# A fixed order for the first keys of an attention and FFN kernel, and its output weights queued behind a copy

## The chip, the cores and the metric

The kernel runs on one core of a Trainium2 chip. A core has five engines that take part: TensorE (PE; its weight loads are shown as PEld), VectorE (DVE), ScalarE (ACT), GpSimd (POOL) and SyncE (SP), which here only issues DMAs. The metric is the device time of one execution in microseconds (us); lower is better.

## What is computed

The reference, cut to what matters:

```python
def attention(hidden_q, hidden_kv, mask, bias):         # h = 32 heads of dh = 128
    q = (hidden_q @ Wq).reshape(b, lq, h, dh)
    k = (hidden_kv @ Wk).reshape(b, lk, h, dh)
    v = (hidden_kv @ Wv).reshape(b, lk, h, dh)
    score = einsum('bqhd,bkhd->bhqk', q, k) / sqrt(dh) + bias
    probs = where(mask, softmax(where(mask, score, -inf)), 0)
    return einsum('bhqk,bkhd->bqhd', probs, v).reshape(b, lq, h * dh) @ Wo

def ffn(x):                                             # 8 experts of rank 16
    base_out = x @ base_W.T + base_b
    topk_p, topk_i = top_k(softmax(x @ router_W.T + router_b), 8)
    w = sum_over_k(topk_p * onehot(expert_map[topk_i]))
    return base_out + einsum((x @ A) * w, B) * 2

x = x + attention(layernorm(x), ctx, mask, bias)        # x, ctx: 16 x 64 x 512, fp32
x = x + ffn(layernorm(x))
```

There are 1024 tokens of width 512. The weights Wq, Wk and Wv are 512 x 4096, Wo is 4096 x 512.

## The kernel before

**Products.** Every large fp32 product is made from two halves of each operand: `split` (L69-71) casts the source to a reduced fp32 on ScalarE (the high part, names ending in `h`) and subtracts it from the source on VectorE (the low part, names ending in `l`). `mm3` then issues three matmuls, high by high, low by high and high by low (L262). On top of it the projections of queries, keys and values use a form of Winograd's scheme: both operands are cut into 2 x 2 blocks, and seven products of sums of blocks take the place of eight products of blocks. `winograd` (L213-257) issues the products in the order 1, 2, 6, 5, 7, 4, 3. The sums of token blocks are made by `Tokens.make` (L136-146; names `tt`, `t1` to `t7`), those of key weights by `Weights.make` (L164-173; `s`, `gh`, `gl`), those of value weights by `OctWeights.make` (L198-206). Product 6 needs two sums on each side (s1, then s2), 5 uses the first of them, 7, 4 and 3 need a third or fourth. After a product, `post` copies PSUM banks on ScalarE (`u`, `u2`, `u3`, `c21`) or adds them on VectorE (`c11`, `c22`, `c12`), and the results are stored in DRAM by DMA (`kd` for keys, `vd` for values).

**Stages.** A quad is four heads. The first stage makes the keys of quads 0 and 1 together. Their seven products are interleaved, quad 0 then quad 1; one product of one quad is 12 matmuls of 128 x 512. Product 1 is written out by hand on TensorE, VectorE and ScalarE (from L360). For the other six, the loop at L411-421 makes the operands of the next product for quad 0, for the tokens and for quad 1, and then steps both quads. There only TensorE's order is fixed as written (`manual_schedule` from L355). VectorE's and ScalarE's orders are made by the framework's scheduler. Then come stages of values (eight heads at a time) and of keys, each with its operands made a stage ahead. The loads of key weights use the buffers `raw` (ten), those of value weights the buffers `o` (nine), which the token sums `tt` use too.

**Pairs.** Sixteen pairs of heads follow. Each does the scores of its two heads (`S`), seven products of the queries of the next pair (`Q`), the output projection of the previous pair (`O`) and transposes of the probabilities (`T`). The string of steps is `QSQQOOQOQOOQOQOTTO`, and a pair ends with the products of probabilities and values. `scores` (L484-504) runs 16 exponentials on ScalarE for the two heads. The `Queries` products 1, 6 and 7 are copied out of PSUM by `u` (L558, ScalarE); the bank of products 1, 6, 7 and 4 is the same, so a following product cannot write it before the copy. `load_o` (L468-476) loads the two blocks of output weights of the pair (`so`, 256 KB each) and splits them into `wh` and `wl`; it stands at the third `Q` (L610-611).

**Order.** [...] Outside of `manual_schedule` the scheduler sets it from the order of the program, dependencies and its own estimates. `tc.issue_after(x)` adds an order edge: what is issued under it comes after x.

Of the kernel before, what the change touches and what calls it, by code (L numbers as in the profile page):

```python
# [15 lines left out]
ALU = mybir.AluOpType  # L16
# [20 lines left out]
ORDER = (1, 2, 6, 5, 7, 4, 3)  # L37
# [10 lines left out]
def xattn_ffn_kernel(ctx: ExitStack, tc: tile.TileContext, x, ctxT, wq, wk, wv, wo, fside, mask,  # L48
                     base_wT, base_b, arT, router_b, lora_b, expert_map, out):
    nc = tc.nc  # L50
# [58 lines left out]
    with ExitStack() as actx:  # L109
# [9 lines left out]
        class Tokens(dict):  # L119
# [13 lines left out]
                    r.append(d)  # L133
                return r

            def make(self, i):  # L136
                b, t = self.b, self.t
                if i == 6:
                    t[1] = self.diff(b[0, 1], b[0, 0], "tt1")
                    t[2] = self.diff(b[1, 1], t[1], "tt2")  # L140
                src = (b[0, 0] if i == 1 else b[1, 0] if i == 2 else t[2] if i == 6 else t[1] if i == 5 else
                       self.diff(b[1, 1], b[0, 1], "tt3") if i == 7 else
                       self.diff(b[1, 0], t[2], "tt4") if i == 4 else b[1, 1])
                self[i] = [tp.tile([P, 2, HALF], F32R, tag=f"t{i}{c}", name=f"t{i}{c}") for c in "hl"]
                for k in range(2):
                    split(self[i][0][:, k], self[i][1][:, k], src[k])
# [6 lines left out]
        class Weights(dict):  # L153
# [7 lines left out]
                self.eng.tensor_tensor(r, a, b, op)  # L161
                return r

            def make(self, i):  # L164
                a11, a12, a21, a22 = self.a
                if i == 6:
                    self.s1 = self.summed(a21, a22, ALU.add, "s1")
                    self.s2 = self.summed(self.s1, a11, ALU.subtract, "s2")
                src = (a11 if i == 1 else a12 if i == 2 else self.s2 if i == 6 else self.s1 if i == 5 else
                       self.summed(a11, a21, ALU.subtract, "s3") if i == 7 else a22 if i == 4 else  # L170
                       self.summed(a12, self.s2, ALU.subtract, "s4"))
                self[i] = [blk("g", f"g{c}", F32R, (P, 2, self.cols)) for c in "hl"]
                split(self[i][0], self[i][1], src)

# [5 lines left out]
        class OctWeights(dict):  # L180
# [25 lines left out]
                    split(self[i][0][kc], self[i][1][kc], src[kc])  # L206

            def all(self):
                for i in ORDER:
                    self.make(i)  # L210
                return self

        def winograd(mm, n, emit, yzbank=bank, order=ORDER, begun=None):  # L213

            xb, zb, yb, u, u2, u3 = ({} for _ in range(6))

            def post(i, k):
                if i == 1:  # L220
                    u[k] = blk("sn", "u")
                    nc.scalar.copy(u[k], xb[k])
                elif i == 2:
                    c = blk("ob", "c11")
                    nc.vector.tensor_tensor(c, u[k], zb[k], ALU.add)
                    emit(0, 0, k, c)
                elif i == 6:
                    u2[k] = blk("sn", "u2")
                    copied[:] = [nc.scalar.copy(u2[k], xb[k])]
                elif i == 7:  # L230
                    u3[k] = blk("sn", "u3")
                    copied[:] = [nc.scalar.copy(u3[k], xb[k])]
                    c = blk("ob", "c22")
                    nc.vector.tensor_tensor(c, u3[k], yb[k], ALU.add)
                    emit(1, 1, k, c)
                elif i == 4:
                    c = blk("ob", "c21")
                    nc.scalar.copy(c, xb[k])
                    emit(1, 0, k, c)
                elif i == 3:  # L240
                    c = blk("ob", "c12")
                    nc.vector.tensor_tensor(c, u2[k], yb[k], ALU.add)
                    emit(0, 1, k, c)

            for i in order:
                for k in range(n):
                    if i == 1:
                        xb[k] = begun[k] if begun else bank()
                    elif i == 2:
                        zb[k] = yzbank(k)  # L250
                    elif i == 5:
                        yb[k] = yzbank(k)
                    b = xb if i in (1, 6, 7, 4) else zb if i == 2 else yb
                    if i > 1 or not begun:
                        mm(i, k, b[k], i in (1, 2, 5))
                    post(i, k)
                yield i

        def mm3(o, stat, mov, first, last):
# [83 lines left out]
        def emit_k(q):  # L343
            def emit(i, j, k, c):
                stored[:] = [nc.sync.dma_start(out=kd[4 * q + 2 * i + k][:, j * HALF:(j + 1) * HALF], in_=c)]
            return emit
# [8 lines left out]
        with tc.manual_schedule(engines={nc.tensor.engine}):  # L355
# [3 lines left out]
            with tc.manual_schedule(engines={nc.tensor.engine, nc.vector.engine, nc.scalar.engine}):  # L359
# [22 lines left out]
                for q in range(2):  # L382
                    part(q, 1)
                    begin(q, 1)
            both = [winograd(mm_weights(tc_, gs[q]), 2, emit_k(q), yz, begun=xbs[q]) for q, yz in
                    enumerate((bank, lambda k: small_bank("yz")))]

            def keys_of(q, g):
# [19 lines left out]
                    q, kind = stages[n]  # L408
                    ops[n] = gran4(load_raw(wk[q]), nc.vector) if kind == "k" else OctWeights(wv[q // 2])

            for n in range(7):  # L411
                if n < 6:
                    gs[0].make(ORDER[n + 1])
                    tc_.make(ORDER[n + 1])
                    gs[1].make(ORDER[n + 1])
                else:
                    load(0)
                    load(1)
                    ops[0].all()
                next(both[0])  # L420
                next(both[1])
            for n, (q, kind) in enumerate(stages[:-1]):
                load(n + 2)
                ops[n + 1].all()
# [115 lines left out]
            class Queries:  # L540
# [6 lines left out]
                def run(self, g, order):  # L547
                    mm = mm_weights(tx, g)
                    b, s = {}, {}
                    for i in order:  # L550
                        x_ = "x" if i in (1, 6, 7, 4) else "z" if i == 2 else "y"
                        if i in (1, 2, 5):
                            b[x_] = bank()
                        mm(i, 0, b[x_], i in (1, 2, 5))
                        with tc.high_priority(offset=SOON):
                            if i in (1, 6, 7):
                                s[i] = blk("sn", "u")
                                nc.scalar.copy(s[i], b["x"])  # L558
                            if i == 4:
                                self.blocks[1, 0] = blk("ob", "q21")  # L560
                                nc.scalar.copy(self.blocks[1, 0], b["x"])
                            for at, key, u, bk in ((2, (0, 0), 1, "z"), (7, (1, 1), 7, "y"), (3, (0, 1), 6, "y")):
                                if i == at:
                                    self.blocks[key] = blk("ob", "q")
                                    add = nc.vector.tensor_tensor(self.blocks[key], s[u], b[bk], ALU.add)  # L565
                                    if i == 7:
                                        self.last = add.ins
                        yield
# [24 lines left out]
            for p in range(NP):  # L593
# [7 lines left out]
                for c in steps:  # L601
                    if c == "S":
                        ps = [scores(qs.head(i), ks[i], bms[i]) for i in range(2)]
                        if not last:
                            ks = [load_k(2 * p + 2 + i) for i in range(2)]
                            bms = [bias_of(2 * p + 2 + i) for i in range(2)]
                    elif c == "Q":
                        nxt(1)
                        n += 1
                        if n == 3:  # L610
                            w = load_o(p)
                        if n == 7 and p + 2 < NP:
                            with tc.issue_after(nxt.last):
                                after = Queries(load_pair(p + 2), ORDER)
                        if n == 7 and p + 2 == NP:
                            sar = [blk("raw", "sar", F32, (P, 2, NB)) for _ in range(2)]
                            sbw = [blk("raw", "sbw") for _ in range(KC)]
                            slb = blk("g", "slb")
                            nc.sync.dma_start(out=slb, in_=lora_b)
                            for i in range(2):  # L620
                                nc.gpsimd.memset(sar[i][:, :, NAR:NB], 0.0)
                                nc.sync.dma_start(out=sar[i][:, :, 0:NAR], in_=arT[:, 2 * i:2 * i + 2])
                            for kc in range(KC):
                                nc.sync.dma_start(out=sbw[kc], in_=base_wT[:, kc])
                    elif c == "T":
                        pts.append(transpose_p(ps[len(pts)]))
                    else:
                        proj_o(t, *prev)
                        t += 1
                        if last and t == 2:  # L630
                            w = load_o(p)
# [221 lines left out]
```

## Time and profile before

| what | us |
|---|---|
| median of three runs (lowest, highest) | 779.36 (778.44, 779.77) |
| the profiled execution | 779.6 |
| its span, first to last instruction | 777.8 |
| TensorE busy in the span | 769.8 |
| VectorE busy | 573.5 |
| ScalarE busy | 413.8 |
| GpSimd busy | 134.3 |

The mean granted TensorE clock was 0.998 of full speed. A line of the timeline reads: start, duration, engine, line of the kernel, operation, output and inputs, shape; in brackets the idle time of the engine before it and what ended it. The names in the lines are the program's tile names. A DMA's time to landing is counted from its issue.

### The profile page before, as it was taken

To read this page: it belongs to the slowest core of one execution; us is meant where nothing else is said; L and a number is where in the kernel's file an instruction comes from. 1 tells how busy PE (TensorE), PEld (TensorE's weight loads), DVE (VectorE), ACT (ScalarE), POOL (GpSimd) and SP (SyncE) were. 2 spreads that over 40 slices of the span, in tenths; PEclk is the share of its full clock that TensorE was granted. 3 is DMA by queue.
4 is the path that set the end of the run, shared out by engine and by line. 5 is a ranking of instruction groups with operands and counts; after the bars stand their busy time and mean duration, and the time that the engine had idled before them with its cause. 6 is when DMAs were issued, how large, how long until landed. Compare 5 with 4: busy or idle time off the path is not lost.

```text
span 777.8 us, 16657 instructions
## 1 busy us (share of the span) xinstructions
PE 769.8 (99%) x6306; PEld 641.6 (82%) x6306; DVE 573.5 (74%) x1037; ACT 413.8 (53%) x1166; POOL 134.3 (17%) x143
## 2 busy tenths in 40 slices
PE   8999999999999999999999999999999999999998
PEld 5888888888888888878888888888888888888897
DVE  7995566566665756788878787778777877779975
ACT  5654454545544545576564556555655565556461
POOL 0000000000000522133320332033203320210330
PEclk9999999999999999999999999999999999999999
DMA  7595646464634445574543354425542544252011
GB/s 260 192 304 177 203 154 210 134 212 151 205 119 175 150 141 198 166 245 140 184 164 126 103 180 164 140 93 177 163 143 93 175 164 143 98 170 69 1 56 55
DMA packets 74993, 120.48 MB, mean 155 GB/s; under 512 B 7712, under 2 KB 25376, under 8 KB 74912
## 3 DMA queue, kind: packets, MB, share of 16 engines
q1 hardware_dynamic: 74768, 119.36, 46.1%
q8 instruction: 49, 0.80, 0.4%
q14 instruction: 32, 0.26, 0.1%
q10 hardware_dynamic: 144, 0.06, 0.0%
HBM read 83.74 MB, written 35.65 MB: 153 GB/s over the span
## 4 chain that ended last, share of the span: by engine, by line
PE 95%; DVE 3%; DMA 1%; SPq 0%; ACT 0%; issue 0%; POOL 0%; DVEq 0%; POOLq 0%
PE ps L262 75%; PE yz L262 5%; PE ps L699 5%; PE pss L490 4%; PE ps L522 4%; PE pst L509 2%; DVE gl L71 1%; DMA cT<-in_ctxT 1%; PE pst L104 0%; DVE bs L665 0%; PE pt L104 0%; DVE tt L132 0%; DVE ol L71 0%; DVE s L161 0%; POOL st L668 0%
## 5 line engine op out<-in xcount | busy, mean ns | idle before, releaser
L70 ACT CAST gh<-s 128x512 fp32r<-128x512 f32 (+1 forms) x128 | 65.5, 515 | 90.7 <-PE ps L262 81.8
L498 ACT ACTIVATE p<-p,nm 128x64 f32<-128x64 f32 x256 | 85.5, 336 | 30.8 <-DVE nm L495 30.8
L262 PE MATMUL ps<-wh,oh 128*128 128x512 f32 x256 | 101.3, 396 | 0.0
L538 DVE TENSOR_TENSOR acc<-acc,ps 128x512 f32<-128x512 f32 x128 | 86.8, 681 | 19.2 <-PE ps L262 19.0
L71 DVE TENSOR_TENSOR gl<-s,gh 128x512 fp32r<-128x512 f32 (+1 forms) x128 | 71.6, 563 | 39.7 <-ACT gh L70 39.1
L262 PE MATMUL ps<-wh,ol 128*128 128x512 f32 x256 | 99.8, 390 | 0.0
L262 PE MATMUL ps<-wl,oh 128*128 128x512 f32 x256 | 99.8, 390 | 0.0
L161 POOL TENSOR_TENSOR s<-rq 128x256 f32<-128x256 f32 x32 | 26.1, 815 | 261.7 <-DMA rq<-in_wq 128.0
L71 DVE TENSOR_TENSOR gl<-raw,gh 128x512 fp32r<-128x512 f32 (+1 forms) x49 | 34.6, 705 | 35.4 <-ACT gh L70 25.0
L70 ACT CAST gh<-raw 128x512 fp32r<-128x512 f32 (+1 forms) x49 | 29.8, 609 | 57.2 <-PE yz L262 36.6
L262 PEld LDWEIGHTS ps<-wl,oh 128*128 128x128 f32 x256 | 48.0, 188 | 10.0
L262 PEld LDWEIGHTS ps<-wh,ol 128*128 128x128 f32 x256 | 48.1, 188 | 9.8 <-DVE ol L71 0.5
L262 PEld LDWEIGHTS ps<-wh,oh 128*128 128x128 f32 x256 | 48.1, 188 | 9.5
L481 POOL TENSOR_TENSOR bm<-bm,maskb 128x512 f32<-128x512 f32 x32 | 49.2, 1558 | 29.4 <-DVE rc L502 22.0
L498 ACT ACTIVATION_READ_ACCUMULATOR p<-p,nm 128x1 f32 x256 | 48.2, 188 | 0.0
L71 DVE TENSOR_TENSOR ol<-ps,oh 128x512 fp32r<-128x512 f32 x64 | 39.9, 683 | 10.2 <-ACT oh L70 10.2
L96 POOL TENSOR_TENSOR rs<-rs,nhalf 128x1 f32<-128x1 f32 x8 | 4.4, 549 | 246.1 <-DVE rs L95 240.8
L558 ACT COPY u<-ps 128x512 f32<-128x512 f32 x48 | 27.7, 578 | 32.9 <-PE ps L262 32.8
L70 ACT CAST oh<-ps 128x512 fp32r<-128x512 f32 x64 | 33.2, 591 | 11.6 <-PE ps L522 11.6
L565 DVE TENSOR_TENSOR q<-u,ps 128x512 f32<-128x512 f32 x48 | 32.6, 680 | 8.8 <-PE ps L262 8.8
L503 DVE TENSOR_TENSOR p<-p,rc 128x512 f32<-128x512 f32 x32 | 36.6, 1143 | 1.1
L71 DVE TENSOR_TENSOR wl<-so,wh 128x512 fp32r<-128x512 f32 x32 | 36.6, 1143 | 0.7 <-ACT wh L70 0.7
(262 smaller groups left out, 2006.1 us busy)
## 6 DMA issues: line engine op xcount, KB each, us to landing
kd<-c SPq DMA_DIRECT2D x64, 256.0 KB, 2.2
vd<-c SPq DMA_DIRECT2D x64, 256.0 KB, 2.6
kT<-kd SPq DMA_DIRECT2D x64, 256.0 KB, 4.7
v<-vd SPq DMA_DIRECT2D x64, 256.0 KB, 4.1
raw<-in_wv SPq DMA_DIRECT2D x32, 256.0 KB, 4.2
rq<-in_wq SPq DMA_DIRECT2D x32, 256.0 KB, 4.5
bm<-in_fside SPq DMA_DIRECT2D x32, 256.0 KB, 4.9
so<-in_wo SPq DMA_DIRECT2D x32, 256.0 KB, 2.6
```

The costliest lines, as they stand in the source:

```text
L70: nc.scalar.copy(hi, src)
L71: (lo_eng or nc.vector).tensor_tensor(lo, src, hi.bitcast(F32), ALU.subtract)
L262: nc.tensor.matmul(o, lhsT=a, rhs=b, start=first and n == 0, stop=last and n == 2, skip_group_check=True)
L481: nc.gpsimd.tensor_tensor(bm, bm, maskb, ALU.add)
L490: nc.tensor.matmul(ps[a * S:(a + 1) * S, t, :], lhsT=qT[n // 8][:, c], rhs=kT[n // 8][:, c], start=True, stop=True)
L498: nc.scalar.activation(p[:, t, :], p[:, t, :], AF.Exp, bias=nm[:, t:t + 1], accum_out=sme[:, t:t + 1])
L503: nc.vector.tensor_tensor(p, p, rc.unsqueeze(2).to_broadcast([P, NT, S]), ALU.mult)
L522: nc.tensor.matmul(ps[b][d:d + S, u * S:(u + 1) * S], lhsT=v[u // 2][r, u % 2, c], rhs=pt[r, u, :], start=True, stop=True)
L538: nc.vector.tensor_tensor(acc[:, t, :], acc[:, t, :], ps, ALU.add)
L558: nc.scalar.copy(s[i], b["x"])
L565: add = nc.vector.tensor_tensor(self.blocks[key], s[u], b[bk], ALU.add)
L699: nc.tensor.matmul(o, lhsT=a, rhs=b, start=start, stop=stop, skip_group_check=True)
```

## The change

The change has two parts.

1. `Tokens.make` and `Weights.make` are cut in two, `sums` (the additions) and `make` (the splits). `winograd` gets an argument `late`, which puts a yield between a product's matmuls and its `post`. With both, products 2 to 7 of the first stage are written out in one order that holds on TensorE, VectorE and ScalarE alike. The operands of the value stage's products 1 and 2 (`ops[0].make(1)`, `make(2)`) stand in this order too, and `rest(2)` makes the other five.
2. In `Queries`, the first copy `u` is remembered, and `load_o` is issued after it.

```diff
-            def make(self, i):
+            def sums(self, i):
...
+            def make(self, i, src=None):
+                src = src or self.sums(i)
...
             def all(self):
-                for i in ORDER:
+                return self.rest(0)
+
+            def rest(self, n):
+                for i in ORDER[n:]:
                     self.make(i)
                 return self
...
-                    post(i, k)
+                    if not late:
+                        post(i, k)
+                if late:
+                    yield
+                    for k in range(n):
+                        post(i, k)
                 yield i
...
-            for n in range(7):
-                if n < 6:
-                    gs[0].make(ORDER[n + 1])
-                    tc_.make(ORDER[n + 1])
-                    gs[1].make(ORDER[n + 1])
-                else:
-                    load(0)
-                    load(1)
-                    ops[0].all()
-                next(both[0])
-                next(both[1])
+            fixed = {nc.tensor.engine, nc.vector.engine, nc.scalar.engine}
+            with tc.manual_schedule(engines=fixed):
+                def go(*qs):
+                    for q in qs:
+                        next(both[q])
+
+                gs[0].make(2)
+                tc_.make(2)
+                gs[1].make(2)
+                go(0, 0, 0, 1, 1, 1)
+                t6 = tc_.sums(6)
+                gs[0].make(6)
+                tc_.make(6, t6)
+                gs[1].make(6)
+                go(0, 0)
+                tc_.make(5)
+                gs[0].make(5)
+                go(1, 1, 0, 0)
+                gs[1].make(5)
+                go(1, 1)
+                tc_.make(7)
+                gs[0].make(7)
+                go(0, 0)
+                gs[1].make(7)
+                go(1, 1)
+                tc_.make(4)
+                gs[0].make(4)
+                go(0, 0)
+                gs[1].make(4)
+                go(1, 1)
+                tc_.make(3)
+                gs[0].make(3)
+                go(0, 0)
+                load(0)
+                load(1)
+                ops[0].make(1)
+                gs[1].make(3)
+                go(1, 1)
+                ops[0].make(2)
+                go(0, 1)
+            ops[0].rest(2)
...
                                 s[i] = blk("sn", "u")
-                                nc.scalar.copy(s[i], b["x"])
+                                copy = nc.scalar.copy(s[i], b["x"])
+                                if i == 1:
+                                    self.first = copy.ins
...
-                            w = load_o(p)
+                            with tc.issue_after(nxt.first):
+                                w = load_o(p)
```

More of the change, by code (lines that the diff above doesn't have):

```diff
@@ L140, in make @@
                     t[2] = self.diff(b[1, 1], t[1], "tt2")
-                src = (b[0, 0] if i == 1 else b[1, 0] if i == 2 else t[2] if i == 6 else t[1] if i == 5 else
-                       self.diff(b[1, 1], b[0, 1], "tt3") if i == 7 else
-                       self.diff(b[1, 0], t[2], "tt4") if i == 4 else b[1, 1])
+                return (b[0, 0] if i == 1 else b[1, 0] if i == 2 else t[2] if i == 6 else t[1] if i == 5 else
+                        self.diff(b[1, 1], b[0, 1], "tt3") if i == 7 else
+                        self.diff(b[1, 0], t[2], "tt4") if i == 4 else b[1, 1])
+            def make(self, i, src=None):
+                src = src or self.sums(i)
                 self[i] = [tp.tile([P, 2, HALF], F32R, tag=f"t{i}{c}", name=f"t{i}{c}") for c in "hl"]
@@ L162, in summed, with sums @@
                 return r
-            def make(self, i):
+            def sums(self, i):
                 a11, a12, a21, a22 = self.a
@@ L168, in make @@
                     self.s2 = self.summed(self.s1, a11, ALU.subtract, "s2")
-                src = (a11 if i == 1 else a12 if i == 2 else self.s2 if i == 6 else self.s1 if i == 5 else
-                       self.summed(a11, a21, ALU.subtract, "s3") if i == 7 else a22 if i == 4 else
-                       self.summed(a12, self.s2, ALU.subtract, "s4"))
+                return (a11 if i == 1 else a12 if i == 2 else self.s2 if i == 6 else self.s1 if i == 5 else
+                        self.summed(a11, a21, ALU.subtract, "s3") if i == 7 else a22 if i == 4 else
+                        self.summed(a12, self.s2, ALU.subtract, "s4"))
+            def make(self, i):
+                src = self.sums(i)
                 self[i] = [blk("g", f"g{c}", F32R, (P, 2, self.cols)) for c in "hl"]
@@ L208, in all, with winograd @@
             def all(self):
-                for i in ORDER:
+                return self.rest(0)
+            def rest(self, n):
+                for i in ORDER[n:]:
                     self.make(i)
                 return self
-        def winograd(mm, n, emit, yzbank=bank, order=ORDER, begun=None):
+        def winograd(mm, n, emit, yzbank=bank, order=ORDER, begun=None, late=False):
             xb, zb, yb, u, u2, u3 = ({} for _ in range(6))
@@ L384, in xattn_ffn_kernel @@
                     begin(q, 1)
-            both = [winograd(mm_weights(tc_, gs[q]), 2, emit_k(q), yz, begun=xbs[q]) for q, yz in
+            both = [winograd(mm_weights(tc_, gs[q]), 2, emit_k(q), yz, begun=xbs[q], late=True) for q, yz in
                     enumerate((bank, lambda k: small_bank("yz")))]
```

## The prediction

> **What bounds the kernel now.** I read the page first (busy shares, then the chain of waits), then TensorE's waits over the whole run, then the timeline, windows and chain at the two places where these waits stand.
>
> The page:
>
> ```profile
> PE 769.8 (99%) x6306; PEld 641.6 (82%) x6306; DVE 573.5 (74%) x1037; ACT 413.8 (53%) x1166; POOL 134.3 (17%) x143
> ...
> PE 95%; DVE 3%; DMA 1%; SPq 0%; ACT 0%; issue 0%; POOL 0%; DVEq 0%; POOLq 0%
> ```
>
> TensorE bounds it: 99% busy, 95% of the chain. Only TensorE's stalls, and what is slow at start and end, can be won. All of its listed waits of 0.3 us or more (total, times, longest):
>
> ```profile
> PE ps L262 <- ACT gh L70: 1.4, 1, 1.4
> PE warm L358 <- DVE zero L84: 1.0, 1, 1.0
> PE ps L262 <- ACT u L558: 1.0, 1, 1.0
> PE ps L262 <- DVE gl L71: 0.6, 1, 0.6
> ```
>
> The change can touch three of them: `gh` and `gl` (both at product 6 of quad 0, near 17 us) and `u` (second pair, near 348 us). Timeline of product 6[...] (PE, PEld, DVE, ACT, POOL busy, then the clock):
>
> ```profile
> 17.10 0.69 DVE L161 TENSOR_TENSOR s<-raw 128x512 f32<-128x512 f32 x1
> 17.21 0.62 ACT L70 CAST gh<-s 128x512 fp32r<-128x512 f32 x1 [1.74 <-DVE s L161]
> 17.70 0.68 DVE L225 TENSOR_TENSOR c<-u,ps 128x512 f32<-128x512 f32 x1
> ...
> 17.89 0.50 PE L262 MATMUL ps<-t6h,gh 128*128 128x512 f32 x1 [1.36 <-ACT gh L70]
> ...
> 18.30 0.68 DVE L71 TENSOR_TENSOR gl<-s,gh 128x512 fp32r<-128x512 f32 x1
> ```
> ```profile
> 16.50:19.90 3.40, 1.39 (x6) 0.92 (x6) 3.40 (x7) 0.90 (x2) 0.00 (x0) 1.00 0.65 226
> 19.90:23.30 3.40, 3.40 (x10) 2.66 (x9) 3.36 (x6) 1.44 (x3) 0.00 (x0) 0.50 0.41 156
> ```
>
> VectorE works without a gap (a 0.68 us operation starts every 0.60) while TensorE waits, and half the clock follows. The rest of the stage in the chain (start, length, what):
>
> ```profile
> 31.60 13.60 PE ps L262 x60
> 45.20 2.72 PE yz L262 x12
> 47.92 8.16 PE ps L262 x36
> ```
>
> Twelve matmuls, one product of one quad, take 2.72 us (0.2267 each), and the stage ends at 47.92 (product 3 of quad 1). The last operand of it was made long before:
>
> ```profile
> 40.94 0.69 DVE L71 TENSOR_TENSOR gl<-s,gh 128x512 fp32r<-128x512 f32 x1
> ```
>
> So VectorE is then about 3.6 us ahead (41.63 against 45.20). The second pair:
>
> ```profile
> 347.56 0.62 ACT L70 CAST wh<-so 128x512 fp32r<-128x512 f32 x1 [2.34 <-DVE ol L71]
> 348.09 0.58 ACT L558 COPY u<-ps 128x512 f32<-128x512 f32 x1
> 350.32 0.35 ACT L498 ACTIVATE p<-p,nm 128x64 f32<-128x64 f32 x1 [1.66 <-DVE nm L495]
> ```
>
> The cast is not late because of `ol`, as the wait says: its transfer was issued at 343.55 and took 3.9 us (the DMA list), so it landed at 347.46. The copy that TensorE needs stood behind it; TensorE went on at 348.72.
>
> [...] Here the clock is 0.50 for one window only, but the window before it is 41% busy (1.39 of 3.40)[...]. [...]
>
> **Part 1: the fixed order of the first stage.** It adds no instruction. TensorE's and GpSimd's orders stay the same in the whole program; VectorE's, ScalarE's and SP's change up to about 75 us. What goes: product 6's operand moves forward on VectorE. Before, its sums s1, s2 stood between t6l and c11; now s1 is first as soon as its data are there. The DMA list puts the last needed piece of `wk` at 14.72, so: s1 14.75, s2 at 15.47 to 16.15, cast 16.18 to 16.80, t6h 17.32, first matmul at 17.38 where it was 17.89; gl comes in step. In all TensorE lost 4.18 us here: 1.53 to gh, 0.92 to gl, 0.11 at the restart, 1.62 to eleven matmuls at half clock (4.11 us instead of 2.49). After the change I find it 2.1 us ahead when product 5 begins.
>
> What comes: the order is rigid on VectorE. In six quad-operands (s2 and s3 of both quads, s4 of both) a sum is followed by its own low part, which waits for ScalarE's cast between. Sum 0.69, cast 0.62 and 0.06 of hand-over make 1.37 where VectorE's pitch is 0.60: a gap of 0.77. The trace shows this gap once:
>
> ```profile
> 23.93 0.62 ACT L70 CAST gh<-s 128x512 fp32r<-128x512 f32 x1
> ...
> 24.58 0.69 DVE L71 TENSOR_TENSOR gl<-s,gh 128x512 fp32r<-128x512 f32 x1 [1.27 <-ACT gh L70]
> ```
>
> Before, the scheduler filled it elsewhere with additions and the low parts of tokens. In the new order I count 43 starts on VectorE from s1 to the gl of product 3, quad 1 (with two low parts of the value weights and two sums s8 of the next stage put ahead of that gl): 43 x 0.60 = 25.8. Gaps: s2 twice 0.12 + 0.77, tt3 and tt4 0.18 each, s3 twice 0.78, s4 of quad 0 0.78, and 0.91 where the value weights' casts stand on ScalarE behind the two copies c21: 5.4 together. s4 of quad 1 has no gap, the s8 sums lie in it. So gl starts at 14.75 + 25.8 + 5.4 = 45.95, ends near 46.65. TensorE's lead melts: 2.1 us at product 5, 0.9 at 7 and 4; product 3 of quad 0 is 0.4 late, that of quad 1 gets gh at 45.54 and gl at 46.67, then 11 matmuls of 0.2267 and 0.1: 49.27. Against 47.92 that is **+1.35 us**. The value stage's operands come with slack (its first products' weights are cast before, its product 6 is needed near 60 and made near 52), so neither recovers nor adds anything: TensorE is full from there.
>
> On SP eight loads of `wv` go into buffers of token sums; the seventh and eighth stand behind stores of c22 that are ready near 38.3. In the DMA-heavy stretch 30 to 46 a `wv` transfer took 4.3 us median, so they land at 43 to 45 by this. The s8 sums at 44.74 and 45.34 wait for them: cost 0 if they land in time, up to +1 if not. I take 0; below nothing isn't possible, as the sums only stand ahead of gl.
>
> **Part 2: output weights behind the query's first copy.** Same casts and subtractions; both wh casts now stand right after copy u and before the 16 exponentials (before: one ahead of u, one after the exponentials); on VectorE wl of the second moves forward, on SP the bias load swaps place with a kT load. In the second pair u no longer waits: product 6 starts at 347.57 instead of 348.72, **-1.15**. But wh of the second weight waits for its transfer, issued at 346.04, 5.6 us: 351.6. Behind it are all exponentials: from 352.2 instead of 350.32. The second copy is 4 exponentials later, done 354.1 and needed at 354.4 (covered by 0.3); the third is done at 358.99 and needed at 358.45, **+0.55**. Net -0.6. Other pairs have no such stall in the waits; there the second cast waits for nothing but the copy and puts the exponentials some 1.2 us later (near 478 us: 478.6 instead of 477.37); the transposes that need them come ten us later (494), so 0.
>
> **Sum.** +1.35 - 0.6 = +0.75 on the profiled execution, 779.6 us (span 777.8 and 1.8 around it): 780.35. The median shown is 0.24 lower, 779.36: **780.1**.
>
> **Rivals.**
> - Faster. VectorE's gaps don't bind: the lead of 2.1 at product 5 is kept because a gap is smaller than I make it, or the engine catches up (before it was 3.6 us ahead at the end, and 5.4 of gaps exceed this by only 1.8). And u's 1.15 is kept. 779.36 - 2.1 - 1.15 = 776.1. For it: TensorE's two waits and the half clock are real, 4.18 us. Against: 43 starts on one engine leave no room.
> - Slower, one mechanism: the last gl's lateness. TensorE stands still at 44.93 to 45.54 and 46.04 to 46.67, 1.24 us; if the s8 transfers come after 45.3, gl moves with them and this grows. [...] 780.1 + 1.8 = 781.9.
> - Part 2 gives nothing: the transfer, not the place in the queue, rules, and what u gains the exponentials lose (-1.15, +1.15). 779.36 + 1.35 = 780.7.
>
> **How the numbers follow.** Forecast 0.47 (own range 779.0 to 781.3), faster 0.26, slower 0.20, part 2 nothing 0.07. 0.2% is 1.56 us, about what a measurement tells from no change: below 777.8 is faster, above 780.9 slower. Faster: 0.26 and 0.03 of the forecast's tail, 0.29. Slower: 0.20, 0.09 of the tail, 0.03 of the last: 0.32. Same 0.39. The range takes in the faster case's 776.1 with some margin and the slower one: 775.8 to 782.3.
>
> **What would show it.** TensorE's waits should have gh near 17 us down from 1.4 to about 0.9, u L558 gone at 348, and new waits of 0.6 and 0.6 for product 3's gh and gl near 45 to 47; VectorE's waits for casts should come to about 5 us before 47 us. The chain should enter product 3 of quad 1 from VectorE, and its end should be at 49.3. If TensorE never waits after product 6 and the stage ends before 47.9, the first step is wrong and the time is under 778. If s8 waits for a DMA at 45 or a second window shows half clock, the slower case holds. In the second pair the exponentials should start near 352.2; if at 350 my transfer time is wrong.

## The result and the profile after

| | before | changed |
|---|---|---|
| median, us (lowest, highest) | 778.93 (776.65, 780.64) | 781.41 (779.96, 783.31) |
| profiled execution | 779.6 | 780.15 |
| its span | 777.8 | 778.1 |
| its mean TensorE clock | 0.998 | 1.000 |

Ten executions each; the ratio is 1.0033 with a 95% interval of 1.0018 to 1.0048. The change made the kernel 2.5 us slower, more than the 0.75 that the prediction's sum gave. The two profiled spans differ by 0.3 only. The explanation below has to cover both: the traces agree with the sum step by step, and the medians don't.

TensorE's six longest waits in the changed kernel (total, times, longest):

```profile
PE warm L373 <- DVE zero L84: 1.0, 1, 1.0
PE ps L277 <- ACT t6h L70: 0.9, 1, 0.9
PE yz L277 <- DVE gl L71: 0.8, 1, 0.8
PE yz L277 <- ACT gh L70: 0.6, 1, 0.6
PE ps L277 <- DVE gl L71: 0.4, 2, 0.2
PE ps L277 <- ACT u L603: 0.3, 1, 0.3
```

The wait of 1.4 us at product 6 is down to 0.9 (`t6h`). The wait for the first copy near 348 us is gone, and 0.3 us for the third copy has come. The two waits with `yz` are new: product 3 of quad 1 stands still twice. The chain of waits, near the end of the first stage (start, length, what), says why:

```profile
38.60 1.20 DVE t3l L71 x2
39.81 0.61 DVE s L164
40.55 0.42 issue
40.97 0.59 ACT c L248
41.58 2.84 DMA kd<-c
44.44 0.63 DVE s L199
45.11 0.69 DVE s L199
45.80 0.61 DVE gl L71
46.46 2.83 PE yz L277 x11
49.29 8.16 PE ps L277 x36
```

Before, this stretch of the chain was TensorE alone and the stage ended at 47.92. Now it runs over VectorE and ends at 49.29. The two sums `s` of line 199 belong to the next stage's value weights; they stand ahead of the last `gl`. They are no part of the written order (`rest(2)` stands behind it); the framework's scheduler put them there. The name `kd<-c` of the transfer has to be read with care. The sums read no keys; they wait for loads of `wv`, and the last of those was issued at 40.26 and took 4.7 us (the DMA list), so it landed at 44.96, just ahead of the second sum at 45.11. The trace of a second measurement of the changed kernel (below) names the load itself: its chain has `39.64 5.10 DMA raw<-in_wv` ahead of the first sum at 44.83.

VectorE's own waits from 14 to 56 us:

```profile
DVE gl L71 <- ACT gh L70: 4.2, 6, 0.8
DVE s L164 <- DMA raw<-in_wk: 0.2, 1, 0.2
```

Before, VectorE waited for casts 1.8 us in all from 14 to 48 us, three times. The fixed order has six, each about 0.7: five sums followed by their own low parts (0.69 each), and 0.80 at the value weights.

### The profile page after: what moved, and what is told of

It is laid out like the page before. It is cut to its first block, busy times and chain, and to the rows that moved or that the text cites. A ratio compares the mean times of both kernels' runs of the same rounds, so it can differ in the third digit from the quotient of the medians.

```text
span 778.1 us, 16653 instructions
## 1 busy us (share of the span) xinstructions
PE 769.7 (99%) x6306; PEld 639.5 (82%) x6306; DVE 565.4 (73%) x1037; ACT 413.5 (53%) x1166; POOL 131.3 (17%) x143
## 4 chain that ended last, share of the span: by engine, by line
PE 90%; DVE 4%; DMA 2%; ACT 2%; issue 0%; SPq 0%; POOL 0%; DVEq 0%; ACTq 0%; POOLq 0%
PE ps L277 70%; PE ps L747 5%; PE yz L277 5%; PE ps L567 4%; PE pss L535 4%; PE pst L554 2%; DVE gl L71 1%; DMA so<-in_wo 1%; ACT p L543 1%; DMA raw<-in_wk 1%; DMA cT<-in_ctxT 1%; DVE s L164 1%; PE pst L104 0%; ACT gh L70 0%; DVE bs L713 0%
## 5 line engine op out<-in xcount | busy, mean ns | idle before, releaser
L526 POOL TENSOR_TENSOR bm<-bm,maskb 128x512 f32<-128x512 f32 x32 | 45.9, 1453 | 29.3 <-DMA bm<-in_fside 29.3
L548 DVE TENSOR_TENSOR p<-p,rc 128x512 f32<-128x512 f32 x32 | 39.4, 1231 | 1.1
L70 ACT CAST wh<-so 128x512 fp32r<-128x512 f32 x32 | 19.9, 621 | 34.7 <-PE ps L277 29.5
```

Source lines behind the costliest of these rows:

```text
L70: nc.scalar.copy(hi, src)
L526: nc.gpsimd.tensor_tensor(bm, bm, maskb, ALU.add)
L548: nc.vector.tensor_tensor(p, p, rc.unsqueeze(2).to_broadcast([P, NT, S]), ALU.mult)
```

## The experiments

**Do the clock and the span vary in the kernel before?**

> The kernel before, unchanged, to see the clock and span of each of its executions. My theory: the loss at half clock near 20 us, which I counted against the kernel before as a part of every execution, stands in some of them only: executions with a clock of 0.998 have spans near 777.8 us, those with 1.000 near 776.2 (1.6 less). Rival: every execution shows 0.998, the half clock is there each time and doesn't explain why the change measured slower than its profile says.

They vary, and 1.4 us lie between the first two groups where I expected 1.6. The kernel was copied without an edit: 778.96 us against 778.8, ratio 1.0005 (0.9997 to 1.0012). Taken together with the executions of the kernel before that ran beside the other experiments, there are 141 with a clock in the record. In the trace before, the clock is 0.50 from 19.88 to 23.30, for 3.41 us. Such a window lowers the mean clock of a 778 us span by about 0.002 (half of 3.41 over 778), and the profiled executions agree: the one before, with one window, has 0.998, this copy, with two, 0.996. So I take the number of an execution's windows from its mean clock (an estimate):

| clock | before: executions, median span | changed: executions, median span |
|---|---|---|
| 0.999 to 1.000 | 40, 775.8 | 15, 778.5 |
| 0.997, 0.998 | 82, 777.2 | 8, 780.65 |
| 0.996 (one at 0.994) | 19, 778.4 | none |

So by this count most executions of the kernel before have one window and are 1.4 us longer, some have two and are 2.6 longer, and more than a quarter have none. That the windows lie near product 6 is read from two profiled traces (half clock from 19.88 in the trace before, from 18.11 in this copy); and since a longer wait goes with the half clock (2.1 us for `gh` in this copy, 1.4 in the trace before, 0.9 for `t6h` in the changed kernel, which has none there), not all of the 1.4 need be the clock's. The profiled trace of this copy has two windows. Its windows there (PE, PEld, DVE, ACT, POOL busy, then the clock):

```profile
14.70:18.11 3.41, 1.33 (x7) 0.80 (x5) 3.41 (x7) 1.69 (x4) 0.00 (x0) 1.00 0.81 265
18.11:21.52 3.41, 3.01 (x7) 2.02 (x8) 3.41 (x7) 0.62 (x1) 0.00 (x0) 0.50 0.34 130
21.52:24.94 3.42, 3.42 (x10) 2.65 (x9) 1.91 (x4) 1.76 (x4) 0.00 (x0) 0.50 0.30 116
```

TensorE is 39% busy in the first (1.33 of 3.41 us), and the next two run at half; in the trace shown with the prediction it was 41% busy in the stretch ahead of the half clock. In that trace half clock begins a second time behind TensorE's last instruction, at 777.64, which is 757.76 us after 19.88; in 222 equal steps that is 3.413 us each, the length of the first. In the changed kernel's trace it begins once, at 778.90. Counted back from there in the same steps (an estimate from these two traces), the window at product 6 is 14.31 to 17.73. Product 6 starts earlier in it, TensorE is 73% busy (2.50 us), and the clock stays at 1.00 behind it.

The same trace corrects a second number. Its second pair has no wait for `u`:

```profile
347.63 0.62 ACT L70 CAST wh<-so 128x512 fp32r<-128x512 f32 x1 [1.21 <-DVE gl L71]
348.15 0.58 ACT L558 COPY u<-ps 128x512 f32<-128x512 f32 x1
```

The casts of TensorE's results ahead of them (`oh`) come 1.2 us later there than in the trace before (345.33 instead of 344.13). Yet the cast and the copy come at the same times (347.56 and 348.09 before), since ScalarE waited 1.21 us ahead of the cast instead of 2.34, and TensorE has no wait listed from 340 to 365 us. The stall of 1.0 us belonged to the one profiled execution in which the load took 3.9 us. The two other traces without part 2 below list no wait for `u` either.

**Each part alone.** In the first of these the edit of `load_o` is undone, in the second only that edit is made:

```diff
-                            with tc.issue_after(nxt.first):
-                                w = load_o(p)
+                            w = load_o(p)
```

> Part 1 alone. My theory (VectorE's gaps bind): the first stage ends near 49.3 us as in the changed kernel, the second pair waits for u again (1.0), so the span of an undisturbed execution is 0.9 above the changed kernel's 778.1, near 779.0, and the ratio to before 1.004. Rival (the slowdown comes from part 2 or its order of transfers): the ratio is 1.002 or less.

> Part 2 alone. My theory: the wait for u near 348 us goes, a smaller one for the third copy comes, net 0.6 to 0.9 us less, ratio 0.999. Rival (the exponentials behind the second cast delay the pair, in other pairs too): no gain or a loss, ratio 1.000 to 1.002, and new waits of TensorE after 350 us.

The fixed order alone: 780.62 us, ratio 1.0032 (1.0019 to 1.0045), all of the change's loss. The wait for `u` that I expected in it didn't come (ScalarE waited 1.03 us ahead of the cast of `wh` there, instead of 2.34), and its spans at full clock, 778.3 to 778.6, are no longer than the changed kernel's. The weights behind the copy alone: 778.97 us, ratio 1.0002 (0.9992 to 1.0011); of the expected gain, 0.6 us lies at the edge of the interval and 0.9 outside. That expectation missed. The ratio is the rival's, but not its cause: the trace shows no new wait of TensorE from 350 us on.

The trace of the fixed order alone caught what the profiled execution of the changed kernel had not. VectorE and TensorE at the end of its first stage:

```profile
45.75 1.36 DVE L199 TENSOR_TENSOR s<-raw,raw 128x512 f32<-128x512 f32 x2 [0.72 <-DMA kd<-c]
47.03 0.68 DVE L71 TENSOR_TENSOR gl<-s,gh 128x512 fp32r<-128x512 f32 x1
...
47.77 0.77 PE L277 MATMUL yz<-t3h,gl 128*128 128x512 f32 x1 [1.54 <-DVE gl L71]
48.34 0.63 PE L277 MATMUL yz<-t3l,gh 128*128 128x512 f32 x1
48.77 0.63 PE L277 MATMUL yz<-t3h,gh 128*128 128x512 f32 x1
```
```profile
44.41:47.82 3.41, 1.29 (x6) 0.51 (x4) 2.69 (x6) 2.63 (x5) 0.00 (x0) 1.00 1.01 375
47.82:51.23 3.41, 3.41 (x8) 2.73 (x9) 3.41 (x6) 0.62 (x1) 0.00 (x0) 0.50 0.95 341
```

Here the sums of line 199 waited 0.72 us for a load of `wv` (the DMA list: 5.5 us to landing); the last `gl` moved with them, and the window was 38% busy. The next ran at half clock (0.50), with eight matmuls where the one from 37.59 to 41.00, at full clock, has 17. This is the prediction's slower rival, in all its parts. The span of this execution is 780.8; those at 1.000 have 778.3 to 778.6. Both parts count in the difference: the wait for `gl` is 1.54 us instead of 0.78, and the eleven matmuls behind it take 4.22 us (47.77 to 51.99) instead of 2.83 (46.46 to 49.29).

**Is the half clock near 48 us what the slower executions lose?** Twelve matmuls of zeros were put into TensorE's idle time, with their output going to a bank already copied out; nothing reads it.

```diff
                 gs[1].make(3)
-                go(1, 1)
+                go(1)
+                for _ in range(WARM):
+                    nc.tensor.matmul(xbs[0][0][:, 0:256], lhsT=zero[:, 0:P], rhs=zero, start=True, stop=True)
+                go(1)
```

> The changed kernel with 12 small matmuls of zeros ahead of product 3 of quad 1 on TensorE; they write a bank that was copied out before, and nothing reads them. They shorten no wait for gh or gl; they only fill TensorE's idle time near 45 us. Theory of the half clock (idle time near 45 to 47 halves the clock in some executions and costs 1.5 to 2 us then): most executions show 0.999 or 1.000, spans near 778.1 to 779, median near 780.3, some 1 us below the changed kernel's 781.4. Rival (the slower executions come from later transfers alone): clocks of 0.998 as often as before, 4 of 10, or gone without the time falling.

> The changed kernel, unchanged, to see the clock of more of its executions beside the kernel with covered idle time (2 of 21 below 0.9985). My theory: 3 to 6 of 10 executions show 0.998 with spans of 779.5 to 781.5, the others 778 to 779.2; median 780.3 to 781.5. Rival (the half clock comes as seldom as with the cover): at most 1 of 10.

With the cover 19 of 21 executions are at 0.999 or above, and the median is 780.52, ratio 1.0025 (1.0017 to 1.0032). The wait for `gl` is still 0.8 us, and with the zeros TensorE is 75% busy in this stretch and the clock stays at 1.00 behind it:

```profile
44.40:47.80 3.40, 2.56 (x18) 1.82 (x17) 2.89 (x6) 2.63 (x5) 0.00 (x0) 1.00 1.00 375
47.80:51.20 3.40, 3.40 (x17) 2.77 (x16) 3.40 (x7) 0.62 (x1) 0.00 (x0) 1.00 0.87 309
```

The changed kernel again: 780.87, with 4 of 13 at 0.998 (4 of 10 in the first measurement). So 2 of 21 with the cover stand against 8 of 23 without it. This is no clear difference: another variant without the cover, measured beside it on the same chip (the second block behind the exponentials, below), has 4 of 19. What does differ is the long spans: none of the 21 is over 779.6, while 6 of the 23 and 3 of the 19 are over 780. The medians, 780.52 and 780.87, are too close to size it that way. By clock, the changed kernel's spans are 780.65 and 778.5, a difference of 2.1 us. That is more than I estimate for one window at half clock (half of its 3.41 us, 1.7), so it holds the later transfer too; the trace above splits it into 1.4 at half clock and 0.8 of wait. That the half clock adds to the later transfer is shown by that trace; how much of the medians it carries isn't shown by the cover.

**The place of the value weights.**

```diff
-                ops[0].make(1)
                 gs[1].make(3)
+                ops[0].make(1)
```

> The changed kernel with one pair of lines exchanged: the operand of product 3 of quad 1 stands ahead of the value weights, and so ahead of the two sums that wait for transfers of value weights; all gaps but the last stay. My theory: the last gl no longer waits for the value weights' casts (0.8), two low parts, two sums and a transfer; it ends near 44 us instead of 46.4, TensorE doesn't stand still there, the stage ends at 47.2 to 47.6 instead of 49.3, no execution shows half clock near 48, and the median falls by 2 to 3 us, ratio to before 0.999 to 1.001. Rival (the gaps themselves carry the loss, the place of the value weights doesn't matter): the stage still ends after 48.5 and the ratio stays above 1.002.

778.74 us, ratio 1.0000 (0.9992 to 1.0009), with 13 of 14 executions at full clock. This exchange alone gives the loss back. The stage ends a little later than I expected, at 48.29 instead of 47.2 to 47.6. VectorE (timeline) and the chain show what is left:

```profile
42.04 0.69 DVE L71 TENSOR_TENSOR gl<-s,gh 128x512 fp32r<-128x512 f32 x1 [0.69 <-ACT gh L70]
42.65 0.69 DVE L164 TENSOR_TENSOR s<-raw,s 128x512 f32<-128x512 f32 x1
44.02 0.69 DVE L71 TENSOR_TENSOR gl<-s,gh 128x512 fp32r<-128x512 f32 x1 [0.69 <-ACT gh L70]
45.26 0.69 DVE L199 TENSOR_TENSOR s<-raw,raw 128x512 f32<-128x512 f32 x1 [0.54 <-DMA raw<-in_wv]
```
```profile
42.79 2.79 PE ps L277 x11
45.57 2.72 PE yz L277 x12
48.29 8.16 PE ps L277 x36
```

The last `gl` ends at 44.71, ahead of 45.57. Now quad 0's `gl` at 42.04 sets the end (the chain enters TensorE from it at 42.79): VectorE's gaps still bind, one product earlier.

**The gaps filled.** The sums stand a step earlier, so that other VectorE work lies between a sum and its low part, and the value weights come last. The core of it:

```diff
                 t6 = tc_.sums(6)
-                gs[0].make(6)
+                a = gs[0].sums(6)
                 tc_.make(6, t6)
-                gs[1].make(6)
+                gs[0].make(6, a)
+                a = gs[1].sums(6)
                 go(0, 0)
+                gs[1].make(6, a)
...
+                a = [g.sums(3) for g in gs]
                 tc_.make(3)
-                gs[0].make(3)
-                go(0, 0)
+                for g, s in zip(gs, a):
+                    g.make(3, s)
+                go(0, 0, 1, 1)
```

Products 7 and 4 are treated alike (t7, s3 and t4 ahead of the splits).

> The changed kernel with the same operations, the sums standing one step earlier, so that another VectorE operation lies between each sum and its own low part, and the value weights behind product 3. My theory (5.4 us of gaps on VectorE bind): VectorE's waits for casts fall from 4.2 to under 1 us, product 3 of quad 1 waits for nothing, and the first stage ends at 44.5 to 45.5 instead of 49.3: about 4 us below the changed kernel, ratio to before 0.997 or less. Rival (transfers or ScalarE bind behind the gaps): the stage ends at 47 us or later and TensorE's waits have other names.

776.45 us, ratio 0.9970 (0.9959 to 0.9982), all six executions at full clock. VectorE's waits from 14 to 56 us no longer hold a cast:

```profile
DVE s L200 <- DMA raw<-in_wv: 1.8, 1, 1.8
DVE s L164 <- DMA raw<-in_wk: 0.7, 1, 0.7
DVE c L245 <- ACT u L243: 0.6, 1, 0.6
```

and the chain leaves VectorE at 21 us:

```profile
20.43 0.61 DVE gl L71
21.05 0.04 issue
21.09 5.51 PE ps L278 x23
26.61 2.72 PE yz L278 x12
29.33 13.60 PE ps L278 x60
42.93 2.72 PE yz L278 x12
45.65 8.16 PE ps L278 x36
```

The stage ends at 45.65, just behind the expected 44.5 to 45.5 and 3.64 us earlier than in the changed kernel, of which the exchange alone gave 1.00; the sums for the value weights wait 1.8 us for their load and nothing waits for them.

**Part 2 on top of it.** Three kernels say what the weights' place is worth when VectorE's gaps in the first stage are filled. In one, part 2 stands as in the change; in one it is undone; in one (tried also on the changed kernel itself) only the first block stays behind the copy, and the second goes behind the last exponential:

```diff
-                    split(hl[0], hl[1], s)
+                    if first is None:
+                        split(hl[0], hl[1], s)
+                    else:
+                        with tc.issue_after(exps[-1] if i else first):
+                            split(hl[0], hl[1], s)
```

> The gaps filled, and part 2 undone. TensorE has no clock loss in the first stage there, so what part 2 is worth shows with less scatter. My theory (part 2 removes a wait that only some executions have, and puts a smaller one in its place): 0 to 0.5 us above the kernel with gaps filled and part 2, in the same call. Rival (part 2 takes away 0.6 us or more in each execution): 0.6 to 1.2 us above it.

> The kernel with the gaps filled and part 2, again, beside the one without part 2: spans of 773.8 to 774.8, median near 776.3, ratio to before 0.997. The rival to it (its first reading was favoured by the chip): 777 or more.

> The changed kernel with the second output weight's split put behind the pair's last exponential, as it stood before; the first one stays behind the query's first copy. My theory (the second cast's transfer holds up the exponentials in the second pair): the wait of 4.6 us on ScalarE goes, exponentials start near 350 us there, the third copy isn't late, and it is 0.3 us faster than the changed kernel, so a median of 780.5 to 781.5. Rival (the exponentials behind it don't matter): the same time within 0.2 us, and TensorE's 0.3 us at u stays.

> The kernel with the gaps filled, and the second output weight's split behind the last exponential. My theory: the two add up, 0 to 0.4 us below the 776.4 of the kernel with the gaps filled alone, ratio to before 0.9965 to 0.997. Rival (in that kernel the second cast covers itself): no difference, or slower.

Filled, without part 2: 776.26, ratio 0.9966 (0.9956 to 0.9977). Filled, with it, on the same chip: 776.82, ratio 0.9978 (0.9970 to 0.9986). My expectation had the order of the two the other way, and the second of them was to come near 776.3; the difference is small, the intervals overlap, and a gain of 0.6 us from part 2 in each execution is excluded. The first stage isn't free of the half clock there: one of nine executions has 0.998, and it is the profiled one. Product 6 waits for `gh` (0.9) and `gl` (0.7) in it, and from 18.29 its chain has 9.81 us for 35 matmuls, where 0.2267 each make 7.93. The second block behind the exponentials: 780.66 on the changed kernel (ratio 1.0027, 1.0020 to 1.0035), and 776.09 on the filled one (0.9966, 0.9955 to 0.9977). Both are within what their comparisons can tell from the kernels without it, so these two are inconclusive. In the trace of the former ScalarE's wait of 4.6 us is gone, but the exponentials start at 351.54 instead of the 350 that I expected: by the trace they waited 3.16 us for the maximum that they subtract (`nm`). TensorE's wait of 0.3 at the third copy is gone from it too, but its spans at full clock have the median 778.6, no less than the changed kernel's 778.5.

The best that was run is the filled order, with, without or with half of part 2: 776.1 to 776.8, 0.2 to 0.3% below the kernel before, and 4 to 5 us below the changed kernel.

## Why the prediction was right and where it was off

The measured 781.41 lies in the range, toward the slow end, and just outside the forecast's own range of 779.0 to 781.3. The chances put "same" (0.39) ahead of "slower" (0.32); slower is what was measured.

*The VectorE count held.* 43 starts and the gaps put the last `gl` at 45.95; it came at 45.72. TensorE was to wait for gh until 45.54 and for gl until 46.67; it went on at 45.19 and 46.46. The stage was to end at 49.27; it ended at 49.29. In between, TensorE was ahead of the kernel before by 2.2 us at product 5 and by 1.0 at 7 and 4, where I had 2.1 and 0.9. Some of the agreement is luck: 0.4 of this lead was there before product 6; product 3 of quad 0, which I had 0.4 late, came 0.6 early; and `gl` was 0.21 early while the eleven matmuls behind it took 2.83 us instead of 2.6. The gaps were predicted at 5.4 in all. The trace lists 4.2, but it counts idle time from an operation's end, and each of the six adds 0.08 against the pitch of 0.60; with the small gaps at s2, tt3 and tt4 (0.6 together) that is 5.3. The chain began at 14.37 instead of 14.75. That the gaps bind is shown by the filled order against the exchange of two lines (the stage ends at 45.65 instead of 48.29, the ratios are 0.9970 and 1.0000), and that the value weights' place carries the last wait, by that exchange. The faster rival, by which the gaps would not bind, is wrong.

*The half clock of the kernel before isn't a constant.* I took the loss of 1.62 us near 20 us as part of the kernel before. By the mean clock it belongs to 101 of 141 executions, and 19 of these have two or three windows. Against an execution without it the stage is not 1.35 us longer but 1.35 + 1.4 = 2.75, with 1.4 from 777.2 - 775.8. The spans at full clock, 775.8 and 778.5, differ by 2.7. The changed kernel has no half clock near 20 us in either of its traces, but pays VectorE's price all the same, since its stage ends by VectorE: TensorE's early lead is waited away. So removing the first stall did what it was meant to, and the gain went into the wait at product 3.

*The slower rival holds in part of the executions.* I gave it 0.20 and treated it as an alternative to the forecast. Its 781.9 counted 1.6 us for a window at half clock, an estimate from the 1.62 that the trace before lost near 20 us. It is an addition to the forecast: 8 of 23 executions of the changed kernel have a window at half clock by their mean clock (0.998), and are 2.1 us longer with the later transfer that goes with it. Where their windows lie isn't on record; in the one trace that shows such a window, that of the fixed order alone, what came ahead of it was what the rival named: a `wv` transfer later than the sum, by 0.72 us. I had taken this wait at 0 between 0 and +1; the profiled executions have about 0 and 0.2 (the changed kernel, twice) and 0.7.

*Part 2 was judged on one execution.* In the profiled one its sum held: against the kernel before, TensorE's matmuls are 1.37 us late ahead of the first copy and 0.08 behind it, a gain of 1.29 where I had 1.15, and 0.69 late behind the third copy, a cost of 0.6 where I had 0.55. The mechanism held too: the second cast waited 4.6 us for its transfer, and the exponentials started late, at 353.55 where I had 352.2. But the stall of 1.15 is there in one trace only, the one that I read, in which the first transfer took 3.9 us. Three others without part 2 (the copy of the kernel before, the fixed order alone, the filled order without part 2) list no wait for `u`; in the first two ScalarE waited 1.21 and 1.03 us ahead of the cast, where it had waited 2.34. The part alone gave 1.0002. Its rival, "gives nothing" (0.07), was nearer the truth in the median.

*The sum, corrected.* Weighted by their numbers, the spans of before give (40 x 775.8 + 82 x 777.2 + 19 x 778.4) / 141 = 777.0, those of the changed kernel (15 x 778.5 + 8 x 780.65) / 23 = 779.2. The difference of 2.3 us is 0.29%, in the interval of the measurement. The time outside of the span adds 0.2: it is 1.8 us in the kernel before and in each part alone, which I had kept, and 2.0 in the changed kernel; why is open. Against the predicted 0.75, the 2.3 are made of: part 1 against an execution with one window, like the one I read, 778.5 - 777.2 = 1.3, where I had 1.35; 0.2 because the average execution of before is 777.0; 0.75 from the late executions (8 of 23, 2.15 each), which I had at 0; and nothing from part 2, where I had -0.6. So most of the difference comes from two terms: the late transfer with its half clock, and part 2's gain. What is not settled is how often an execution of the changed kernel has a window at half clock: 8 did, and only 23 are counted.

## What to carry to other kernels

When an order is fixed by hand on several engines, don't let an instruction follow the one that feeds it by way of another engine: put the next step's independent work between them, and keep what waits for a transfer behind what the bottleneck needs soonest. A stall that half clock follows in one trace is a term with a chance, not a constant (101 of 141 executions of the kernel before had it by their mean clock); look at the clock of several executions before counting it as won. The same holds for a wait on one transfer (the wait for `u` was there in one of four traces without part 2).

## What the hardware showed that I had not expected

Half clock followed stretches in which TensorE had worked. Three stretches of the first stage, at full clock, had half clock behind them: TensorE was 38, 39 and 41% busy in them (the fixed order alone, 44.41 to 47.82; the copy of the kernel before, 14.70 to 18.11; the kernel before, 16.50 to 19.90). Three others had full clock behind them, at 73, 73 and 75% (the changed kernel, 14.31 to 17.73 and, by the same count, 45.03 to 48.45; the kernel with the cover, 44.40 to 47.80). Nothing between 41 and 73% is in these six, and none was made to find where the two part.

Half clock didn't always end after 3.41 us. In the copy of the kernel before, TensorE was 88% busy (3.01 of 3.41 us, 7 matmuls) from 18.11 to 21.52 at half clock, and the next stretch ran at half too. In the kernel before (19.90 to 23.30) and the fixed order alone (47.82 to 51.23) it was busy throughout at half clock, with 10 and 8 matmuls, and full clock followed. The number of matmuls of 128 x 512 in a stretch sorts the first stage's cases as well: 6 or 7 in those with half clock behind them, 8 or more in those with full clock (with the cover 18, of which 12 are its smaller ones of zeros). These are few cases, and why they fall so is not shown.
